# Attention with residual on one Trainium2 core: the second group's tokens turned by VectorE and DRAM, and one query product placed earlier

## The chip, the cores and the metric

The kernel runs on one core of a Trainium2 chip. A core has TensorE (PE in the profile, with its weight loads as PEld), VectorE (DVE), ScalarE (ACT), GpSimd (POOL) and SyncE (SP), which here only starts transfers. Each engine takes its instructions in a fixed order and waits where an operand is not ready. The metric is the time of one execution on the device in microseconds, as a median over runs; lower is better.

## The reference

Multi-query attention over 64 batches of 128 tokens with 512 features, 16 heads of 64, one shared key and value head and one extra "null" key and value per batch. A layer norm stands before and after; the input is added at the end.

```python
xn = layernorm(x, g_in)
q = (xn @ Wq).reshape(b, n, H, DH).transpose(0, 2, 1, 3) * scale
kv = xn @ Wkv
k, v = (kv[..., :DH], kv[..., DH:])
k = jnp.concatenate([nk, k], axis=1)      # null key, null value from cond_64
v = jnp.concatenate([nv, v], axis=1)
sim = jnp.einsum('bhid,bjd->bhij', q, k) + bias
sim = jnp.where(causal_mask, neg, sim)
sim = jnp.where(mask_p[:, None, None, :], sim, neg)
attn = jax.nn.softmax(sim, axis=-1)
out = jnp.einsum('bhij,bjd->bhid', attn, v)
out = out.transpose(0, 2, 1, 3).reshape(b, n, INNER)
return x + layernorm(out @ Wo, g_out)
```

Everything is float32.

## The kernel before

The 64 batches are worked in 16 groups of four (`GB = 4`, 512 tokens) and, for the attention itself, in 32 pairs. The instructions of each engine stand in the order in which the Python code issues them; nothing reorders them. So the lines at the end of the kernel (from line 1559) are a hand-written schedule, first for groups 0 and 1, then `body_first`, then a loop of `turn(d)` and `body(d)` over the pairs. A wait is set wherever an instruction needs a tile that another engine or a transfer writes, or a buffer that another still reads.

*Tokens.* The products need the normed tokens with features on partitions (`xT[g]`, one tile of 2048 columns for a group). There are two ways to get there:

- `norm_T(m)` (line 306), used for the tiles 0 to 7, that is for groups 0 and 1: the tile `x_m` holds one batch; TensorE turns its four 128x128 blocks into PSUM (line 313) and ScalarE copies them out in three pieces (line 315), with two of the four 32-token quarters exchanged.
- `tokens_T(m)`, `tokens_out(g)` and `tokens_in(g)` (lines 321 to 346), used from group 2 on: the tile `x_m` holds a quarter of the tokens of each of the four batches (the load at line 122 picks them). VectorE transposes all 32x32 blocks of the tile (line 326) into a quarter of `xb`, and when four tiles are done one transfer takes `xb` to DRAM (line 335) and four bring it back, 32 partitions each, as `xT` (line 343).

The statistics of a tile's tokens come from VectorE (`norm_stats`, with a power on POOL at line 281), and the norm itself from `norm_apply` (line 293), on ScalarE for the tiles 4 and up (line 302).

*Query products of group 0.* For each of 8 column blocks `c` of `wq` and each half `h` (two batches) of the group there is one product of four accumulating matrix multiplications, into one of two PSUM buffers, "a" for even `c` and "c" for odd. `q_half(c, h)` makes it 256 columns wide; `q_batches(cs)` does the same in two 128-column steps, one batch after the other, for `h = 0`. ScalarE copies the result to `qT` (line 459). The next product of the same parity waits for that copy.

*Bias and scores.* `causal(u)` masks half of the bias on POOL (line 212) and `null_shift(u)` subtracts the null bias on VectorE (lines 225 and 229). `bias_add(b)` on POOL (line 683) makes `s_b`, the bias and mask of a batch. `scores(b, 0)` goes to PSUM tiles of other stages, `scores(b, 1)` of batches 0 and 1 both to the one tile "s" of `ps_s` (line 718). `scores_add` on VectorE (lines 733 and 735) adds them to `s_b`, `scores_max` (line 740) takes maxima, `exps` on ScalarE (line 749) makes one exponential for each of 8 rows of a half, `rinv` (VectorE) and `scale` (POOL, line 771) divide, and `blocks_T` (VectorE, line 787) turns the 32x32 blocks for `values` (line 849).

*Group 1.* From group 1 on the query products are made by Strassen's method: `token_sum(g, k)` on POOL (line 497) and `weight_sum(k)` on VectorE (line 483) prepare sums, `product` (line 515) makes seven products. `body_first` (line 1091) issues those of group 1 for two column blocks `f` at once: after `kv_pair(4)` come the products 1, 2, 5, 6, 7, 4, 3, each for both `f`. Product 6 adds to the PSUM of product 1 and product 7 adds to that of product 6; between them ScalarE copies the running sum out (`keep`, line 527, tiles `kp1`, `ku2`, `ku3`). The order on ScalarE there is: copies of product 1, the keys of `kv_pair_out(4)` (line 390, behind VectorE's value part at line 380), `norm_apply(8)`, copies of product 6 (`ku2`), `norm_apply(9)`, copies of product 7 (`ku3`). `tokens_T(8)` and `tokens_T(9)` stand on VectorE between them.

*Transfers.* Nearly all are issued by SP, in code order. In the stage of the change these are: the value rows `vd` and `vr` (lines 406 and 411), the null value (line 189), the tiles 8 and 9 (line 122), the next mask, `wo` and `gob` (lines 238 and 239).

Of the kernel before, what the change touches and what calls it, by code (L numbers as in the profile page):

```python
# [17 lines left out]
def kernel(  # L18
# [96 lines left out]
    def load_x(m, queue=nc.sync):  # L115
        g, t = divmod(m, GB)
        pool, tag = (rp, "res") if m in (XB + 1, XB + 2) else (xp, "x")
        xs[m] = wM if m == XB else pool.tile([P, DIM], FP, tag=tag, name=f"x_{m}")
        if g < 2:
            queue.dma_start(out=xs[m], in_=x[m])  # L120
        else:
            nc.sync.dma_start(
                out=xs[m], in_=x[g * GB : (g + 1) * GB, t * Q : (t + 1) * Q, :]
            )
# [181 lines left out]
    def norm_T(m):  # L306
        g, t = divmod(m, GB)
        if t == 0:
            xT[g] = gp.tile([P, GB, KC, N], FP, tag="xT", name=f"xT_{g}")
        xh = xs.pop(m)  # L310
        pt = ps_w.tile([P, KC, P], FP, tag="w", name=f"pxT_{m}")
        for kc in range(KC):
            nc.tensor.transpose(pt[:, kc, :], xh[:, kc * P : (kc + 1) * P], ident)
        for at, to, n in ((0, 0, 2), (3, 2, 1), (2, 3, 1)):
            nc.scalar.copy(
                xT[g][:, t, :, to * Q : (to + n) * Q], pt[:, :, at * Q : (at + n) * Q]
            )
# [3 lines left out]
    def tokens_T(m):  # L321

        g, t = divmod(m, GB)
        if t == 0:
            xbs[g] = hp.tile([P, NQ, KC, NQ, Q], FP, tag="xb", name=f"xb_{g}", bufs=1)
        nc.vector.transpose(
            xbs[g][:, :, :, PLACE[t], :].rearrange("p j c q -> p c j q"),
            xs.pop(m).rearrange("p (c j k) -> p c j k", c=KC, k=Q),
        )
# [3 lines left out]
    def tokens_out(g):  # L333
        xds[g] = dp.tile([P, NQ, KC * NQ * Q], FP, tag="xd", name=f"xd_{g}")
        nc.sync.dma_start(
            out=xds[g], in_=xbs.pop(g).rearrange("p j c t q -> p j (c t q)")
        )

    def tokens_in(g):
        xT[g] = gp.tile([P, GB, KC, N], FP, tag="xT", name=f"xT_{g}")  # L340
        xd = xds.pop(g).rearrange("(i p) j e -> j p i e", p=Q)
        for j in range(NQ):
            nc.sync.dma_start(
                out=xT[g][j * Q : (j + 1) * Q].rearrange("p i c n -> p i (c n)"),
                in_=xd[j],
            )
# [81 lines left out]
    def q_tiles(g, fs, tags):  # L428
        units = [(f, h) for f in fs for h in range(2)]
        for (f, h), tag in zip(units, tags):  # L430
            qT[g, f, h] = gp.tile(
                [P, GB // 2, 2, 2, DH], FP, tag=tag, name=f"qT_{g}_{f}_{h}", bufs=1
            )
            q_tags[g, f, h] = tag
# [7 lines left out]
    def q_room(c, h):  # L442
        if c == 0 and h == 0:
            q_tiles(0, range(NF), [f"q{i}" for i in range(2 * NF)])
        return ps_q.tile([P, 2, N], FP, tag="ac"[c % 2], name=f"pq_{c}_{h}")

    def q_mm(pq, c, h, t=slice(0, 2)):
        two = slice(2 * h + t.start, 2 * h + t.stop)
        for kc in (0, 3, 2, 1):
            nc.tensor.matmul(  # L450
                pq[:, t],
                wq[:, kc, c * P : (c + 1) * P],
                xT[0][:, two, kc, :],
                start=(kc == 0),
                stop=(kc == 1),
            )

    def q_copy(pq, c, h):
        nc.scalar.copy(
            q_part(0, c, h), pq.rearrange("p t (h i) -> p t h i", h=2)  # L460
        )

    def q_half(c, h):
        pq = q_room(c, h)
        q_mm(pq, c, h)
        q_copy(pq, c, h)

    def q_batches(cs):
        pqs = [q_room(c, 0) for c in cs]
        for t in range(2):  # L470
            for pq, c in zip(pqs, cs):
                q_mm(pq, c, 0, slice(t, t + 1))
        for pq, c in zip(pqs, cs):
            q_copy(pq, c, 0)

    def weight_sum(k):
        o, p, m, op = {
# [7 lines left out]
    def token_sum(g, k):  # L485

        xS[g, k] = gp.tile([P, GB // 2, HK, N], FP, tag=f"xS{k}", name=f"xS{k}_{g}", bufs=1)
        lo, hi = xT[g][:, 0 : GB // 2], xT[g][:, GB // 2 :]
        b11, b12 = lo[:, :, lo_k], hi[:, :, lo_k]
        b21, b22 = lo[:, :, hi_k], hi[:, :, hi_k]  # L490
        p, m = {
            1: (b12, b11),
            2: (b22, xS.get((g, 1))),
            3: (b22, b12),
            4: (b21, xS.get((g, 2))),
        }[k]
        nc.gpsimd.tensor_tensor(xS[g, k], p, m, ALU.subtract)
# [178 lines left out]
    def bias_add(b, parts=(slice(0, ROW),)):  # L676
        g, t = divmod(b, GB)
        if b < B - 1:
            S[b] = sp.tile([P, R8, ROW], FP, tag="s", name=f"s_{b}", bufs=3)
        else:  # L680
            S[b] = hp.tile([P, R8, ROW], FP, tag="xb", name=f"s_{b}", bufs=1)
        for keys in parts:
            nc.gpsimd.tensor_tensor(  # L683
                S[b][:, :, keys],
                biasp[:, :, keys],
                mneg[:, t, keys]
                .unsqueeze(1)
                .broadcast_to([P, R8, keys.stop - keys.start]),
                ALU.add,
            )  # L690
# [46 lines left out]
    def scores_max(b, hf):  # L737
        if hf == 0:
            nmax[b] = small.tile([P, 2, R8], FP, tag="nmax", name=f"nmax_{b}")
        nc.vector.tensor_reduce(  # L740
            nmax[b][:, hf], S[b][:, :, WITH_NULL[hf]], AX.X, ALU.max, negate=True
        )

    def exps(b, hf, lo=0, hi=R8):
        if hf == 0 and lo == 0:
            rsum[b] = small.tile([P, 2, R8], FP, tag="rsum", name=f"rsum_{b}")
        for k in range(lo, hi):
            row = S[b][:, k, WITH_NULL[hf]]
            nc.scalar.activation(  # L749
                row,  # L750
                row,
                AF.Exp,
                bias=nmax[b][:, hf, k : k + 1],
                accum_out=rsum[b][:, hf, k : k + 1],
            )
# [848 lines left out]
    norm_apply(5)  # L1604
    q_batches((4,))
    norm_apply(6)
    norm_T(4)
    null_shift(1)
    causal(0)
    q_batches((5,))  # L1610
    norm_apply(7)
    norm_T(5)
    mask_neg(0)
    q_batches((6,))
    norm_T(6)
    null_shift(0)
    bias_add(0, (slice(0, UK.start), slice(UK.start, ROW)))
    q_half(7, 0)
    norm_T(7)
    load_null_value()  # L1620
    load_x(8)
    load_x(9)
# [6 lines left out]
    scores_add(0, 1)  # L1629
    scores_max(0, 1)  # L1630
    bias_add(2)
    exps(0, 0, 0, 4)
    q_half(0, 1)
    exps(0, 0, 4)
    q_half(1, 1)
    rinv(0, 0)
    scale(0, 0)
    token_sum(1, 1)
    token_sum(1, 2)
    scores(1, 0, ((ps_y, "X"), (ps_w, "w")))  # L1640
    scores(1, 1)
    scores_add(1, 0)
    scores_max(1, 0)
    scores_add(1, 1)
    scores_max(1, 1)
    exps(0, 1, 0, 4)
    q_half(2, 1)
    exps(0, 1, 4)
    rinv(0, 1)
    scale(0, 1)  # L1650
# [73 lines left out]
```

## Time and profile before

| | |
|---|---|
| median of 3 runs | 1023.34 us (1023.27 to 1023.65) |
| the profiled execution's own time | 1022.89 us |
| its span, first to last instruction | 1021.0 us |
| mean granted TensorE clock | 0.998 |
| transfers | 100.86 MB, mean 99 GB/s |

The busy time of an engine is given as us and as a share of the span; PE's matrix multiplications overlap each other and their ends are modelled. A row of a timeline gives start, length, engine, line, operation, output and inputs, how many instructions are merged into it, and in brackets the idle time ahead of it with what ended it. A row of the chain gives start, length and piece. All times count from the start of the span.

Over the first 120 us, taken in stretches of 10 us, PE is busy all of the time and POOL is busy 10.00, 9.92 and 10.00 us of the stretches from 30 to 60 us. Between 20 and 30 us VectorE is busy 6.33 us and ScalarE 7.74 us.

### The profile page before, as it was taken

To read this page: it belongs to the slowest core of one execution; us is meant where nothing else is said; L and a number is where in the kernel's file an instruction comes from. 1 tells how busy PE (TensorE), PEld (TensorE's weight loads), DVE (VectorE), ACT (ScalarE), POOL (GpSimd) and SP (SyncE) were. 2 spreads that over 40 slices of the span, in tenths; PEclk is the share of its full clock that TensorE was granted. 3 is DMA by queue.
4 is the path that set the end of the run, shared out by engine and by line. 5 is a ranking of instruction groups with operands and counts; after the bars stand their busy time and mean duration, and the time that the engine had idled before them with its cause. 6 is when DMAs were issued, how large, how long until landed. Compare 5 with 4: busy or idle time off the path is not lost.

```text
span 1021.0 us, 31459 instructions
## 1 busy us (share of the span) xinstructions
PE 1013.0 (99%) x12333; PEld 901.6 (88%) x12333; DVE 845.7 (83%) x1958; ACT 673.2 (66%) x2753; POOL 768.6 (75%) x633
## 2 busy tenths in 40 slices
PE   9999999999999999999999999999999999999997
PEld 9888888888888888888888888888988888888886
DVE  6777888888888888888888888888898888977787
ACT  5766677656677665686656776566775657865583
POOL 4997768677686877859678696776868768686686
PEclk9999999999999999999999999999999999999999
DMA  7415243151431415225152340514314152140221
GB/s 218 139 30 150 67 125 111 34 154 63 145 97 69 123 56 152 87 75 140 35 152 85 109 123 29 164 63 138 103 49 134 64 153 89 70 113 24 69 85 62
DMA packets 73835, 100.86 MB, mean 99 GB/s; under 512 B 32212, under 2 KB 36056, under 8 KB 71896
## 3 DMA queue, kind: packets, MB, share of 16 engines
q1 hardware_dynamic: 73392, 98.47, 32.3%
q8 instruction: 96, 1.57, 0.6%
q14 instruction: 51, 0.42, 0.1%
q10 hardware_dynamic: 296, 0.40, 0.1%
HBM read 63.19 MB, written 33.55 MB: 95 GB/s over the span
## 4 chain that ended last, share of the span: by engine, by line
PE 97%; POOL 1%; DVE 1%; issue 0%; ACT 0%; POOLq 0%; DVEq 0%
PE pyX L936 20%; PE pa L515 16%; PE pyY L936 10%; PE pc L515 10%; PE po L849 8%; PE pkv L363 6%; PE pyw L936 5%; PE pl L581 4%; PE pm L647 4%; PE ps L718 3%; PE pq L450 3%; PE sc_X L718 2%; PE sc_Y L718 2%; PE sc_a L718 1%; PE py_s L936 1%; PE busy L1556 1%
## 5 line engine op out<-in xcount | busy, mean ns | idle before, releaser
L749 ACT ACTIVATE s<-s,nmax 128x65 f32<-128x65 f32 (+1 forms) x1024 | 372.1, 369 | 61.7 <-DVE nmax L740 61.7
L771 POOL TENSOR_TENSOR s<-s,rinv 128x512 f32<-128x512 f32 (+1 forms) x132 | 190.6, 1446 | 132.7 <-DVE rinv L767 132.7
L683 POOL TENSOR_TENSOR s<-biasp,mneg 128x1552 f32<-128x1552 f32 (+1 forms) x65 | 206.3, 3177 | 51.0 <-DVE s L733 27.0
L749 ACT ACTIVATION_READ_ACCUMULATOR s<-s,nmax 128x1 f32 x1024 | 197.0, 192 | 0.0
L787 DVE STREAM_TRANSPOSE sb<-s 128x1536 f32<-128x1536 f32 (+1 forms) x68 | 113.6, 1674 | 11.3 <-POOL s L771 11.3
L740 DVE TENSOR_REDUCE nmax<-s 128x8 f32<-128x1032 f32 (+1 forms) x128 | 121.7, 951 | 0.1
L964 ACT COPY y<-pyX 128x256 f32<-128x256 f32 x29 | 10.8, 372 | 167.5 <-PE pyX L936 161.2
L936 PE MATMUL pyX<-wT,oT 128*128 128x256 f32 x464 | 109.8, 380 | 0.0
L936 PE MATMUL pyX<-wo,oT 128*128 128x256 f32 x464 | 109.7, 380 | 0.0
L936 PEld LDWEIGHTS pyX<-wo,oT 128*128 128x128 f32 x464 | 86.2, 191 | 10.4
L936 PEld LDWEIGHTS pyX<-wT,oT 128*128 128x128 f32 x464 | 84.2, 191 | 9.1
L916 POOL TENSOR_TENSOR oT<-oT 128x512 f32<-128x512 f32 x64 | 80.5, 1277 | 3.9 <-PE pyw L936 1.6
L527 ACT COPY ku<-pa 128x256 f32<-128x256 f32 x118 | 43.4, 367 | 59.7 <-issue 30.8
L849 PE MATMUL po<-sb,vr 32*64 32x128 f32 (+1 forms) x3904 | 81.8, 308 | 0.0
L849 PEld LDWEIGHTS po<-sb,vr 32*64 32x64 f32 x3904 | 71.4, 131 | 8.3 <-issue 5.9
L536 DVE TENSOR_TENSOR qT<-pc,ku 128x256 f32<-128x256 f32 x118 | 48.1, 408 | 32.2 <-PE pc L515 19.9
L868 ACT ACTIVATE oT<-po,nv 128x512 f32<-128x512 f32 (+1 forms) x127 | 73.5, 655 | 0.5 <-PE po L849 0.4
L515 PE MATMUL pa<-xS,wq 128*128 128x256 f32 x264 | 67.8, 380 | 0.0
L597 DVE TENSOR_TENSOR qT<-pl,kp 128x128 f32<-128x128 f32 x112 | 32.0, 286 | 42.8 <-PE pl L581 41.9
L281 POOL TENSOR_TENSOR rstd<-rstd,nhalf 128x1 f32<-128x1 f32 x64 | 35.2, 558 | 42.2 <-DVE rstd L280 39.3
L363 PE MATMUL pkv<-xT,wkv 128*128 128x256 f32 x256 | 63.4, 391 | 0.0
L515 PE MATMUL pa<-xT,wq 128*128 128x256 f32 x236 | 60.6, 380 | 0.0
(207 smaller groups left out, 2591.9 us busy)
## 6 DMA issues: line engine op xcount, KB each, us to landing
res<-in_x_dram SPq DMA_DIRECT2D x64, 256.0 KB
out_dram<-y SPq DMA_DIRECT2D x63, 256.0 KB
x<-in_x_dram SPq DMA_DIRECT2D x62, 256.0 KB
xd<-xb SPq DMA_DIRECT2D x14, 1024.0 KB
xT<-xd SPq DMA_DIRECT2D x56, 256.0 KB
vr<-vd SPq DMA_DIRECT2D x64, 128.0 KB
kT<-kT SPq DMA_DIRECT2D x32, 64.0 KB
vd<-vb SPq DMA_DIRECT2D x32, 64.0 KB
```

The lines of the kernel that those rows point to most:

```text
L363: nc.tensor.matmul(pkv, wkv[:, kc, :], xT[g][:, t : t + 2, kc, :], start=(kc == 0), stop=(kc == KC - 1),)
L515: nc.tensor.matmul(prod[tag], w[:, kc, f * P : (f + 1) * P], t[:, :, kc, :], start=(start and kc == 0), stop=(kc == HK - 1), skip_group_ch ...
L683: nc.gpsimd.tensor_tensor(S[b][:, :, keys], biasp[:, :, keys], mneg[:, t, keys] .unsqueeze(1) .broadcast_to([P, R8, keys.stop - keys.start ...
L718: nc.tensor.matmul(home[r][u * DH : (u + 1) * DH, f, :], qT[g, f, t // 2][rows, t % 2, hf, u], kT[rows, 0 : nk // Q, t, :], start=True, st ...
L740: nc.vector.tensor_reduce(nmax[b][:, hf], S[b][:, :, WITH_NULL[hf]], AX.X, ALU.max, negate=True)
L749: nc.scalar.activation(row, row, AF.Exp, bias=nmax[b][:, hf, k : k + 1], accum_out=rsum[b][:, hf, k : k + 1],)
L771: nc.gpsimd.tensor_tensor(sv, sv, rinvs[b, hf][:, lo:hi].unsqueeze(2).broadcast_to([P, hi - lo, sv.shape[2]]), ALU.mult,)
L787: nc.vector.transpose(sbs[b][:, :, lo:hi].rearrange("p j e q -> p e j q"), S[b][:, lo:hi, 1 : ROW - 1].rearrange("p e (j k) -> p e j k", k=Q),
L849: nc.tensor.matmul(po[s][rows, to : to + n], vr[g][quad, t, PLACE[j], :], sb[quad, slots, r * NF : (r + 1) * NF, :], start=(turn == 0), st ...
L868: nc.scalar.activation(to, src, AF.Identity, bias=nv2)
L916: eng.tensor_tensor(o, a, b, op)
L936: nc.tensor.matmul(prod[key], h[:, c, :], w[:, c, :], start=(start and c == 0), stop=(c == HC - 1), skip_group_check=not start,)
```

## The change

Three things change, all before `body_first`.

1. The tiles 4 to 7 of group 1 take the second way to `xT`. Their loads pick a quarter of the tokens of each batch (as those of the later groups do), `norm_T(4..7)` becomes `tokens_T(4..7)`, and `tokens_out(1)` and `tokens_in(1)` stand right behind the last of them, ahead of `null_shift(0)` in the code and ahead of `load_null_value`, `load_x(8)`, `load_x(9)` and `load_late` in SP's queue.
2. The product of block 2 for the second half of group 0, which stood between exponentials behind the scores of batch 1, stands ahead of those scores. The products of the blocks 0 and 1 are made in 128-column steps, and the first of them ahead of `exps(0, 0, 0, 4)`.
3. `token_sum(1, 1)` and `token_sum(1, 2)` stand some lines later in the code; on POOL, whose order they belong to, they keep their place between `scale(0, 0)` and `scale(0, 1)`.

```diff
-        if g < 2:
+        if g == 0:
             queue.dma_start(out=xs[m], in_=x[m])
         else:
             nc.sync.dma_start(
@@
-    def q_batches(cs):
-        pqs = [q_room(c, 0) for c in cs]
+    def q_batches(cs, h=0):
+        pqs = [q_room(c, h) for c in cs]
         for t in range(2):
             for pq, c in zip(pqs, cs):
-                q_mm(pq, c, 0, slice(t, t + 1))
+                q_mm(pq, c, h, slice(t, t + 1))
         for pq, c in zip(pqs, cs):
-            q_copy(pq, c, 0)
+            q_copy(pq, c, h)
@@
     norm_apply(6)
-    norm_T(4)
+    tokens_T(4)
     null_shift(1)
     causal(0)
     q_batches((5,))
     norm_apply(7)
-    norm_T(5)
+    tokens_T(5)
     mask_neg(0)
     q_batches((6,))
-    norm_T(6)
+    tokens_T(6)
+    tokens_T(7)
+    tokens_out(1)
+    tokens_in(1)
     null_shift(0)
     bias_add(0, (slice(0, UK.start), slice(UK.start, ROW)))
     q_half(7, 0)
-    norm_T(7)
     load_null_value()
@@
     bias_add(2)
+    q_batches((0,), 1)
     exps(0, 0, 0, 4)
-    q_half(0, 1)
+    q_batches((1,), 1)
     exps(0, 0, 4)
-    q_half(1, 1)
+    q_half(2, 1)
     rinv(0, 0)
     scale(0, 0)
-    token_sum(1, 1)
-    token_sum(1, 2)
     scores(1, 0, ((ps_y, "X"), (ps_w, "w")))
     scores(1, 1)
@@
     scores_max(1, 1)
+    token_sum(1, 1)
+    token_sum(1, 2)
     exps(0, 1, 0, 4)
-    q_half(2, 1)
     exps(0, 1, 4)
```

The functions that now serve group 1 as well are unchanged:

```python
    def tokens_T(m):
        ...
        nc.vector.transpose(
            xbs[g][:, :, :, PLACE[t], :].rearrange("p j c q -> p c j q"),
            xs.pop(m).rearrange("p (c j k) -> p c j k", c=KC, k=Q),
        )

    def tokens_out(g):
        xds[g] = dp.tile([P, NQ, KC * NQ * Q], FP, tag="xd", name=f"xd_{g}")
        nc.sync.dma_start(
            out=xds[g], in_=xbs.pop(g).rearrange("p j c t q -> p j (c t q)")
        )

    def tokens_in(g):
        ...
        for j in range(NQ):
            nc.sync.dma_start(
                out=xT[g][j * Q : (j + 1) * Q].rearrange("p i c n -> p i (c n)"),
                in_=xd[j],
            )
```

On TensorE, in the query products of group 0's first half (`pq`, the blocks 4 to 7), the order moves like this (`pxT` is the PSUM tile of the transposes, `wM` the tile of `x_4`, `x_202` to `x_206` those of the tiles 5 to 7; lines with + are the changed kernel's):

```order
 L450 MATMUL pq_0_388<-xT_175,wq 128x128 x8
-L313 MATMUL pxT_400<-wR,wM 128x128 x4
-L450 MATMUL pq_0_419<-xT_175,wq 128x128 x8
-L313 MATMUL pxT_430<-wR,x_202 128x128 x4
-L450 MATMUL pq_0_440<-xT_175,wq 128x128 x8
-L313 MATMUL pxT_450<-wR,x_204 128x128 x4
-L450 MATMUL pq_0_463<-xT_175,wq 128x256 x4
-L313 MATMUL pxT_469<-wR,x_206 128x128 x4
+L450 MATMUL pq_0_412<-xT_175,wq 128x128 x8
+L450 MATMUL pq_0_426<-xT_175,wq 128x128 x8
+L450 MATMUL pq_0_450<-xT_175,wq 128x256 x4
```

The 16 transposes are gone; the products follow each other directly, and the scores of batch 0 follow the last product.

On VectorE, between the norm factors of the tiles 5 to 7 and the scores of batch 0, the transposes stand around the two null shifts (`nbp` and `biasp`, lines 225 and 229):

```order
 L289 TENSOR_SCALAR nmr_385<-mv_340,rstd_342 128x1
+L326 STREAM_TRANSPOSE xb_399<-wM 128x4x4x32
 L225 COPY nbp<-nbh 64x8
 L229 TENSOR_TENSOR biasp<-biasp,nbp 64x8x192
+L326 STREAM_TRANSPOSE xb_399<-x_202 128x4x4x32
+L326 STREAM_TRANSPOSE xb_399<-x_204 128x4x4x32
+L326 STREAM_TRANSPOSE xb_399<-x_206 128x4x4x32
 L225 COPY nbp<-nbh 64x8
 L229 TENSOR_TENSOR biasp<-biasp,nbp 64x8x192
```

One transpose comes ahead of `null_shift(1)` and three come ahead of `null_shift(0)`.

In SP's queue, behind the value rows of group 0, the five transfers of the tokens come in:

```order
 L411 DMA vr_376<-vd_373 32x1024 x4
+L335 DMA xd_438<-xb_399 128x2048
+L343 DMA xT_440<-xd_438 32x4x512 x4
 L189 DMA nv_87<-in_cond_dram 64x1 x2
```

The null value and all that follows it in the queue is issued behind the wait of `tokens_in` for the transfer to DRAM.

## The prediction

> **What bounds the kernel now.** I read the page first: its busy shares and the shares of the chain that ended last.
>
> ```profile
> PE 1013.0 (99%) x12333; PEld 901.6 (88%) x12333; DVE 845.7 (83%) x1958; ACT 673.2 (66%) x2753; POOL 768.6 (75%) x633
> PE 97%; POOL 1%; DVE 1%; issue 0%; ACT 0%; POOLq 0%; DVEq 0%
> ```
>
> The chain is TensorE (PE) for 97% of 1021.0 us. So an instruction taken off PE is worth its length, unless PE then reaches something that is not ready. Next the chain in order of time, at the transposes the change removes (columns: start, length, piece).
>
> ```profile
> 22.52 0.43 PE pxT L313 x4
> 22.96 1.79 PE pq L450 x16
> ...
> 29.14 0.44 PE pxT L313 x4
> ...
> 31.07 3.65 PE pq L450 x16
> ...
> 35.35 0.88 PE ps L718 x32
> 36.23 10.56 PE pq L450 x48
> ```
>
> Four groups of transposes (the first and the last are shown) lie end to end with the query products. A product in 128-column pieces takes 1.79 us, one in 256-column pieces 10.56/6 = 1.76, and the two at 31.07 took 3.65.
>
> **What is removed.** 4 x 0.44 = 1.75 us of PE. ACT loses 12 PSUM copies, which frees only ACT. Two products become 128-column ones, 2 x (1.79 - 1.76) = 0.06 us more. If nothing else were late, PE would be 1.7 us ahead.
>
> **What is added on VectorE.** Four block transposes; their price is a row of the same instruction in a later group (the 54.42 row).
>
> ```profile
> 23.56 1.75 DVE L229 TENSOR_TENSOR biasp<-biasp,nbp 64x1536 f32<-64x1536 f32 x1 [1.16 <-POOL biasp L212]
> 25.33 0.53 DVE L225 COPY nbp<-nbh 64x8 f32<-64x8 f32 x1
> 28.06 1.75 DVE L229 TENSOR_TENSOR biasp<-biasp,nbp 64x1536 f32<-64x1536 f32 x1 [2.21 <-POOL biasp L212]
> 54.42 0.71 DVE L326 STREAM_TRANSPOSE xb<-x 128x512 f32<-128x512 f32 x1 [0.79 <-ACT x L302]
> ```
>
> ```profile
> 23.59 2.24 POOL L212 TENSOR_SCALAR_AFFINE_SELECT biasp<-biasp 64x512 f32<-64x512 f32 x1
> 26.94 1.09 POOL L212 TENSOR_SCALAR_AFFINE_SELECT biasp<-biasp 32x1024 f32<-32x1024 f32 x1
> 53.40 1.90 POOL L771 TENSOR_TENSOR s<-s,rinv 128x1024 f32<-128x1024 f32 x1
> 86.30 1.90 POOL L771 TENSOR_TENSOR s<-s,rinv 128x1024 f32<-128x1024 f32 x1 [2.31 <-DVE rinv L767]
> ```
>
> The first transpose (0.71) falls into the 1.16 us before the first null shift, the other three (2.13) into the 2.21 us before the second, where VectorE waits for POOL's causal select. From 25.31 (23.56 + 1.75) they end at 27.44, the copy of 0.53 at 27.97, under POOL's 28.03. The last needs `norm_apply(7)`:
>
> ```profile
> 25.05 0.81 ACT L302 ACTIVATE x<-x,nmr,rstd 128x512 f32<-128x512 f32 x1
> ```
>
> It ends at 25.86, and ACT now reaches it no later. So the transposes cost nothing as long as POOL's select covers them; the margin is 0.06 us. They do not slow POOL: the scale at 53.40 took 1.90 us across one, as did the scale at 86.30. But the small copy at 25.33 ended at 25.86, just after POOL's select (23.59 + 2.24 = 25.83): it seems to have waited for it. In its new place it meets the select that runs to 28.03, so the null shift starts up to 0.1 us late. At the far end, three transposes that all had to wait for POOL would end at 30.2, with the copy 30.7: 2.6 us late. The 54.42 row speaks against that; I take 0.05.
>
> [...]
>
> **The query product moved ahead** covers PE's next wait. The scores of batch 1, second half, need the PSUM that VectorE's add for batch 0 frees.
>
> ```profile
> 33.38 1.22 DVE L735 TENSOR_TENSOR s<-ps,s 128x1024 f32<-128x1024 f32 x1 [0.70 <-POOL s L683]
> ```
>
> That add ends at 34.60, and waits for POOL's bias, not for PE. PE used to reach those scores at 35.35. With 1.75 removed and one product (1.76) put ahead it reaches them near 35.4 again: no stall. Left where it was, the product would have left PE there near 33.6, 1.0 us early. Behind it, each product needs the PSUM copy of the one two before, and those copies stand between exponentials.
>
> ```profile
> 35.97 0.40 ACT L749 ACTIVATE s<-s,nmax 128x129 f32<-128x129 f32 x1
> ...
> 38.45 0.41 ACT L749 ACTIVATE s<-s,nmax 128x129 f32<-128x129 f32 x1
> ...
> 40.01 0.36 ACT L459 COPY qT<-pq 128x256 f32<-128x256 f32 x1
> ...
> 41.64 0.37 ACT L459 COPY qT<-pq 128x256 f32<-128x256 f32 x1
> ```
>
> Four long exponentials take 40.01 - 38.45 = 1.56 us, a copy with the four short ones behind it 41.64 - 40.01 = 1.63. ACT used to start the eight long ones at 35.97, with a copy and a wait among them. Now they run through to 35.97 + 3.12 = 39.1, and product 3 is copied by 39.5; PE wants that buffer at 36.2 + 2 x 1.76 = 39.7. The later copies (by 41.1, 42.8 and 44.6, with the steps above) come 0.4 us or more before PE wants theirs (41.5, 43.2, 46.7). If ACT were 0.5 us slower there, PE would stall, but PE has 1.3 us to lose there before the end notices (below).
>
> **Where the lead is lost.** Ahead of PE's second pair of kept products stands a chain that starts with POOL and VectorE and that the change does not move: transposed blocks of batch 0, a weight sum, the values, then ACT.
>
> ```profile
> 48.20 1.77 DVE L787 STREAM_TRANSPOSE sb<-s 128x1536 f32<-128x1536 f32 x1
> ...
> 52.35 0.49 DVE L380 TENSOR_SCALAR vT<-pkv,nkv 64x256 f32<-64x256 f32 x1
> ```
>
> ```profile
> 52.92 0.76 ACT L390 ACTIVATE kT<-pkv,nkv 64x128 f32<-64x128 f32 x3 [2.27 <-DVE vT L380]
> 53.58 0.81 ACT L302 ACTIVATE x<-x,nmr,rstd 128x512 f32<-128x512 f32 x1
> 54.59 0.37 ACT L527 COPY ku<-pa 128x256 f32<-128x256 f32 x1 [0.20 <-PE pa L515]
> ...
> 56.44 0.36 ACT L527 COPY ku<-pa 128x256 f32<-128x256 f32 x1
> ```
>
> ```profile
> 55.42 0.86 PE pa L515 x4
> 57.14 0.90 PE pa L515 x4
> ```
>
> ```profile
> 56.91 0.73 PEld L515 LDWEIGHTS pa<-xS,wq 128*128 128x128 f32 x4 [0.17 <-issue]
> ```
>
> `body_first` queues on ACT: keys, `norm_apply(8)`, then the copy of `u2`. PE's product 7 adds to the same PSUM and must wait for that copy. The copy waited only 0.20 us for PE, so it can move up by 0.20 (to 54.39) or, if ACT overlaps instructions as at 55.72 to 56.44, to about 54.30. It then ends at 54.67 to 54.76. From the 56.44 copy's end (56.80) PE's weight load began 0.11 later and its product counted from 57.14, 0.34 in all. So product 7 starts at 55.01 to 55.10 instead of 55.42: the 1.7 us shrink to 0.3 or 0.4, and PE waits some 1.3 us there. With the 0.05 of VectorE, **a gain of 0.3 us stays**. Behind this point everything hangs on PE again: POOL, full until then, has 2.80 us to spare.
>
> ```profile
> 82.09 1.90 POOL L771 TENSOR_TENSOR s<-s,rinv 128x1024 f32<-128x1024 f32 x1 [2.80 <-DVE rinv L767]
> ```
>
> **The tokens through DRAM.** SyncE's queue gets five transfers behind the values' four, and the null value, two `x` tiles and the output weights wait behind them.
>
> ```profile
> 26.40 1.73 SPq L411 DMA_DIRECT2D vr<-vd  x4
> 80.03 0.33 SPq L335 DMA_DIRECT2D xd<-xb  x1
> 83.92 0.33 SPq L343 DMA_DIRECT2D xT<-xd  x1
> 88.16 0.63 SPq L406 DMA_DIRECT2D vd<-vb  x1
> 89.24 2.61 SPq L406 DMA_DIRECT2D vd<-vb  x1
> ```
>
> In a later group the way out took 83.92 - 80.03 = 3.9 us; the two `vd` issues waited for the first two returning pieces, so these landed about 4.2 and 5.3 us after 83.92 and the fourth, at 1.1 us a piece, near 7.5. From 28.2 (26.40 + 1.73) that makes 39.6. The reader is POOL's token sum:
>
> ```profile
> 40.63 2.28 POOL L497 TENSOR_TENSOR xS<-xT 128x512 f32<-128x512 f32 x1
> 42.98 2.13 POOL L497 TENSOR_TENSOR xS<-xT,xS 128x512 f32<-128x512 f32 x1
> 45.08 2.88 POOL L771 TENSOR_TENSOR s<-s,rinv 128x1024 f32<-128x1024 f32 x1
> ```
>
> So the trip is hidden with 1 us to spare. PE's own use comes at 36.23 + 10.56 - 1.7 = 45.1, and of the transfers queued behind the first are the `x` tiles, which VectorE reads only after that.
>
> **Sum.** -1.75 + 0.06 + 1.3 + 0.05 = about -0.3 us, made against the profiled execution (1022.89 us, span 1021.0; the median is 1023.34, 0.45 above): **1023.0 us** on the median.
>
> **Rivals.** *The whole lead survives* (0.13): VectorE's chain to the values comes 1.3 us earlier than I think, because ACT finishes the exponentials sooner. For it: ACT has fewer copies. Against it: from 48.20 on the rows lie back to back and start with POOL's scale, not with ACT. It gives 1023.34 - 1.7 = 1021.6. *The null shift slips* (0.12): a transpose more than 0.06 us longer pushes bias, scores and the chain above, and each us of slip is lost one to one; between 0.5 and 1 us this is 1023.5 to 1024.0, in the 2.6 us limit 1025.6. *The tokens land late* (0.07), the slower case: at a landing T POOL needs about 2 x 1.28 + 1.90 us more to finish the scale that VectorE's 48.20 row waits for, with no competing rows by then; it decides from T = 43.5, and T = 45 gives 1023.0 + 1.5 = 1024.5, T = 47 gives 1026.5. Against it: 39.6 is 4 us away. *The change does nothing for PE* (0.03): 1023.3; the order of the instructions shows the transposes gone.
>
> **How the numbers follow.** My forecast, 1022.7 to 1023.3, has 0.65. The range 1021.5 to 1024.4 takes in the surviving lead below and most slips above; beyond it I leave the longest slips and late tokens. A measurement of this kernel tells about 0.2%, 2.05 us, from no change. Faster by more than that needs more than the 1.7 us that are there: 0.05. Slower by more needs the far ends of two rivals: 0.08. Within: 0.87.
>
> **What would show it.** PE's `pxT` rows after 22 us are gone; the scores of batch 0 start near 27.8; the causal null shift starts at 28.1; the copy `ku` at 54.3 to 54.4 follows `norm_apply(8)` with no wait for PE, and PE shows an idle gap of about a microsecond before the seventh product near 55. No such gap, or one in the forties, proves the account wrong; so does a token sum that waits for a transfer.

## The result, and the profile after

| | before | changed kernel |
|---|---|---|
| median, runs side by side (4 and 4) | 1023.48 us (1023.27 to 1023.65) | 1037.68 us (1037.18 to 1040.02) |
| the profiled execution's own time | 1022.89 us | 1037.43 us |
| its span | 1021.0 us | 1035.6 us |
| ratio of the runs | | 1.0143, 95% interval 1.0130 to 1.0156 |

The change costs 14.2 us, 1.4%, far outside the predicted range of 1021.5 to 1024.4.

The page of the changed kernel first: busy shares and the shares of the chain. TensorE's busy time is 3 us longer although it has the same 12333 instructions, and the chain, 97% TensorE before, now has 3% transfers in it.

```profile
PE 1016.0 (98%) x12333; PEld 901.6 (87%) x12333; DVE 846.4 (82%) x1962; ACT 671.1 (65%) x2741; POOL 765.9 (74%) x633
PE 92%; DMA 3%; DVE 2%; POOL 1%; issue 1%; ACT 1%; SPq 0%; POOLq 0%; DVEq 0%; ACTq 0%
```

What TensorE waits for in the changed kernel (line waited for, total us, times, longest). The first three rows are new.

```profile
PE pa L515 <- ACT ku L527: 4.9, 1, 4.9
PE pq L450 <- ACT qT L459: 4.0, 2, 3.4
PE sc_Y L718 <- ACT qT L459: 2.1, 1, 2.1
```

ACT is the releaser only by name, so I followed the wait backwards. First stage, in the changed kernel's timeline of VectorE, ScalarE and POOL (brackets: idle time ahead and what ended it):

```profile
18.08 0.69 DVE L270 BATCH_NORM_STATS2 st<-x 128x6 f32<-128x512 f32 x1 [0.43 <-DMA x<-in_x_dram]
...
20.86 0.69 DVE L270 BATCH_NORM_STATS2 st<-x 128x6 f32<-128x512 f32 x1 [1.68 <-DMA x<-in_x_dram]
...
23.91 0.14 DVE L373 TENSOR_SCALAR nkv<-nkv 64x1 f32<-64x1 f32 x1 [1.95 <-DMA nkv<-in_cond_dram]
```

```profile
24.62 0.76 ACT L390 ACTIVATE kT<-pkv,nkv 64x128 f32<-64x128 f32 x3 [6.12 <-DVE vT L380]
```

```profile
25.68 2.05 PE L450 MATMUL pq<-xT,wq 128*128 128x128 f32 x16 [3.38 <-ACT qT L459]
```

VectorE waits for the tiles of group 1 and then for the null key, a tiny transfer that stands behind those tiles in SP's queue and is issued at 11.56 us in place of 8.83; ScalarE stands 6.12 us behind VectorE with the query copies queued behind its keys; TensorE finds no free PSUM at 22.3. The windows of the same time show why the transfers are late (columns: stretch, length, busy time and count of PE, PEld, DVE, ACT, POOL, granted clock, share of the 16 DMA engines, GB/s). The changed kernel, then the kernel before:

```profile
12.00:14.00 2.00, 2.00 (x20) 2.00 (x19) 0.78 (x2) 0.50 (x2) 0.00 (x0) 1.00 0.34 123
14.00:16.00 2.00, 2.00 (x17) 1.90 (x16) 0.72 (x2) 1.50 (x7) 0.00 (x0) 1.00 0.35 115
```

```profile
12.00:14.00 2.00, 2.00 (x20) 2.00 (x19) 1.20 (x3) 0.72 (x2) 0.00 (x0) 1.00 1.05 389
```

Same bytes to load, a third of the engines at work; the rate for a full share is alike (123/0.34 = 362 GB/s against 389/1.05 = 370), so fewer engines move, and not slower ones. Second stage, around the seventh product, in the changed kernel:

```profile
53.75 0.69 DVE L270 BATCH_NORM_STATS2 st<-x 128x6 f32<-128x512 f32 x1 [3.48 <-DMA x<-in_x_dram]
...
58.19 0.69 DVE L270 BATCH_NORM_STATS2 st<-x 128x6 f32<-128x512 f32 x1 [3.34 <-DMA x<-in_x_dram]
...
59.21 1.77 DVE L787 STREAM_TRANSPOSE sb<-s 128x1536 f32<-128x1536 f32 x1
...
63.27 0.49 DVE L380 TENSOR_SCALAR vT<-pkv,nkv 64x256 f32<-64x256 f32 x1
```

```profile
63.85 0.76 ACT L390 ACTIVATE kT<-pkv,nkv 64x128 f32<-64x128 f32 x3 [7.87 <-DVE vT L380]
```

```profile
59.72 1.03 PE L515 MATMUL pX<-xS,wS 128*128 128x256 f32 x4
65.67 2.04 PE L515 MATMUL pa<-xS,wq 128*128 128x256 f32 x4 [4.92 <-ACT ku L527]
67.51 1.91 PE L515 MATMUL pX<-xS,wq 128*128 128x256 f32 x4
...
72.20 1.03 PE L515 MATMUL pc<-xT,wS 128*128 128x256 f32 x4
```

```profile
60.00:70.00 10.00, 5.08 (x14) 3.85 (x13) 5.76 (x11) 3.45 (x9) 10.00 (x6) 0.75 0.21 64
```

VectorE waits 3.48 and 3.34 us for the tiles 8 and 9; behind them, in the order of its code, stand the blocks of batch 0, the weight sum and the values for ScalarE's keys. TensorE stands 4.92 us. Its granted clock is 0.75 on the mean of these ten us; in windows of 1 us it is 1.00 up to 64 us and 0.50 from 65 to 71, and a product takes 1.91 us in place of 1.03.

The ledger: TensorE's idle gaps are 3.38, 0.65 and 2.15 us in the first stage. At the keys of group 1 (line 363, 46.62 us before) the changed kernel is 5.33 us behind; the three gaps less the 1.75 us of transposes would make 4.4, and the other 0.9 is not taken apart. The gap of 4.92 follows. From 65.67 to 72.20 the four products take 6.53 us where 4 x 0.86 = 3.44 would do (0.86 is the step from one start to the next at 58.86 and 59.72), 3.1 more. That makes 13.35; the first value product (line 849, 63.52 us before) is 13.46 us behind. By 160 us it is 13.8, and so it stays through the loop.

### The profile page after: what moved, and what is told of

Its sections match the earlier page's. It is cut to its first block, busy times and chain, and to the rows that moved or that the text cites. A ratio compares the mean times of both kernels' runs of the same rounds, so it can differ in the third digit from the quotient of the medians.

```text
span 1035.6 us, 31459 instructions
## 1 busy us (share of the span) xinstructions
PE 1016.0 (98%) x12333; PEld 901.6 (87%) x12333; DVE 846.4 (82%) x1962; ACT 671.1 (65%) x2741; POOL 765.9 (74%) x633
## 4 chain that ended last, share of the span: by engine, by line
PE 92%; DMA 3%; DVE 2%; POOL 1%; issue 1%; ACT 1%; SPq 0%; POOLq 0%; DVEq 0%; ACTq 0%
PE pyX L936 19%; PE pa L515 15%; PE pyY L936 10%; PE pc L515 10%; PE po L849 8%; PE pkv L363 5%; PE pyw L936 5%; PE pl L581 4%; PE pm L647 4%; PE ps L718 3%; PE sc_X L718 2%; PE sc_Y L718 2%; DMA x<-in_x_dram 1%; DMA nkv<-in_cond_dram 1%; PE sc_a L718 1%; PE pq L450 1%
## 5 line engine op out<-in xcount | busy, mean ns | idle before, releaser
L515 PEld LDWEIGHTS pa<-xS,wq 128*128 128x128 f32 x264 | 50.9, 194 | 12.5 <-issue 5.3
```

The costliest lines, as they stand in the source:

```text
L515: nc.tensor.matmul(prod[tag], w[:, kc, f * P : (f + 1) * P], t[:, :, kc, :], start=(start and kc == 0), stop=(kc == HK - 1), skip_group_ch ...
```

## The experiments

The kernels of the experiments 1 to 6 were run once each, beside the kernel before at 1022.96 us (1 to 4, one run) or 1023.57 us (5 and 6, median of 9, from 1023.12 to 1025.13), so a difference of a microsecond or two in them is no more than a hint; the others have medians of 4 to 11 runs.

**1 and 2: the form of the loads, in the kernel before.** Tiles 4 to 7 are still one batch each, but the rows are read in 4 pieces of 32, or in 16 pieces of 8 (`n = 16`).

```diff
+        if g == 1:
+            rows, n = x.rearrange("b n e -> (b n) e"), 4
+            each = P // n
+            some = rows[m * P : m * P + n * (each + 1)]
+            some = some.rearrange("(i p) e -> i p e", i=n)[:, 0:each]
+            nc.sync.dma_start(out=xs[m], in_=some)
```

> The kernel before, but the tiles 4 to 7 are loaded as 4 pieces of 32 rows each, with one row skipped between pieces (the same bytes, almost the same place; the output differs, since the tiles hold other rows). Theory 1, the form of the load: a load whose outer dimension is 4 keeps only 4 of 16 DMA engines busy, so the four tiles, the null key and the bias come late as in the changed kernel. In the changed kernel the first bias add started 5.9 us late; expected here 1027 to 1030 us, a DMA share near 0.35 between 12 and 20 us. Theory 2, the trip through DRAM alone is what costs: 1023.0 to 1023.8 us.

> The same, but 16 pieces of 8 rows with one row skipped between pieces (the output differs likewise). If the number of pieces decides (theory 1): 1023.0 to 1023.8 us, DMA share near 1.0 between 10 and 14 us. If it is that the rows do not lie in one run: late as with 4 pieces, 1027 us or more.

Measured: 1029.66 us with 4 pieces, 1023.56 with 16, both as the first theory had it. The windows of the two kernels, 4 pieces first:

```profile
10.00:20.00 10.00, 10.00 (x78) 9.59 (x77) 5.73 (x16) 3.87 (x11) 2.20 (x4) 1.00 0.48 167
20.00:30.00 10.00, 7.01 (x45) 6.78 (x44) 5.57 (x15) 4.40 (x15) 4.62 (x7) 0.74 0.37 95
```

```profile
10.00:20.00 10.00, 10.00 (x77) 9.59 (x76) 7.63 (x22) 4.35 (x14) 3.04 (x5) 1.00 0.98 220
20.00:30.00 10.00, 10.00 (x114) 9.58 (x116) 6.43 (x12) 8.06 (x27) 7.71 (x7) 1.00 0.46 89
```

Nothing differs but the number of pieces that the outer dimension of the read has (and, with it, which rows are skipped). With 4 the DMA share is half (0.48 against 0.98) and TensorE loses 3.0 us by a gap and more by the clock (0.74 from 20 to 30 us); with 16 it is busy throughout. So 6 us of loss need neither transposes nor a trip.

**3: the changed kernel with the loads of tiles 4 to 7 as before** (`if g < 2` at line 119).

> The changed kernel, but the tiles 4 to 7 are loaded as before, one whole batch each (the transposes then put the tokens elsewhere, so the output differs). Theory 1: the stalls of PE before 40 us are gone and the first bias add starts near 30.0 again; what stays is the tiles 8 and 9, which are issued behind the trip and, on 4 engines, land about 14 and 22 us after the transfer to DRAM is issued at 28.2, so VectorE waits about 3 us for the second: 1024 to 1027 us. Theory 2: still 1030 us or more.

Measured: 1028.95 us, between the two theories. The first stage is mended: the scores of batch 0 start 1.81 us earlier than before, the keys of group 1 1.52 us earlier. So the lead that the prediction counted on is there. What is left is the second stage. The first theory had named the tiles 8 and 9, but with a wait of about 3 us; VectorE waits 2.29 and 3.46 us, and TensorE has one gap of 4.4 us and the slow clock behind it (0.93 from 50 to 60 us and 0.90 from 60 to 70, products of 1.78 and 1.91 us). In this kernel's timeline of VectorE:

```profile
46.30 0.69 DVE L270 BATCH_NORM_STATS2 st<-x 128x6 f32<-128x512 f32 x1 [2.29 <-DMA x<-in_x_dram]
...
50.85 0.69 DVE L270 BATCH_NORM_STATS2 st<-x 128x6 f32<-128x512 f32 x1 [3.46 <-DMA x<-in_x_dram]
```

**4: the move of the query product alone, in the kernel before.**

```diff
+    q_batches((0,), 1)
     exps(0, 0, 0, 4)
-    q_half(0, 1)
+    q_batches((1,), 1)
     exps(0, 0, 4)
-    q_half(1, 1)
+    q_half(2, 1)
```

> The kernel before with only the second part of the change: the product of block 2 ahead of batch 1's scores, the blocks 0 and 1 in 128-column steps, the token sums where the change has them. Theory 1: it neither gains nor costs by itself, 1023.0 to 1023.9 us, since PE reaches batch 1's scores 1.7 us later with the same work. Theory 3, the new order of products and copies starves PE: 1025 us or more.

Measured: 1028.84 us, 5 us above the first theory. The third has the number, but not its mechanism: near the edit only 0.8 to 1.6 us were lost (by the starts of the first value product and of the keys behind it). The rest came in small waits of TensorE all along the run, with nothing that the profile shows as releaser. Of the rows below the one at `pa` is another matter, the gap before the seventh product, which the next experiment has too:

```profile
PE pkv L363 <- issue: 1.6, 6, 0.4
...
PE pa L515 <- issue: 0.7, 1, 0.7
PE po L849 <- issue: 0.6, 1, 0.6
```

**5: the same move with 256-column products**, so that TensorE gets as many matrix multiplications as before (`q_half(0, 1)` and `q_half(1, 1)` in the new places).

> The kernel before with the product of block 2 ahead of batch 1's scores, but blocks 0 and 1 made 256 columns wide as before, so that TensorE executes as many instructions as before. The run with 128-column steps had 16 more matmul records, came out at 1028.8 us and lost its time in small stalls without a visible releaser, all along the run. Theory 3a, the count of TensorE's instructions shifts where its instruction stream stalls: 1023.0 to 1024.3 us here, with no such stalls (the later scores of batch 1 may cost up to 1.3 us). Theory 3b, the order itself costs: 1027 us or more.

Measured: 1025.02 us, 0.7 above the expectation; the small waits along the run are gone. There is one gap of 0.8 us before the seventh product; the first value product starts 0.92 us late, and the one run is 1.5 us above the median before. Without a lead of TensorE the moved product delays the scores of batch 1 (36.78 us in place of 35.17) and all that VectorE does behind them.

**6: the changed kernel with whole-batch loads for the tiles 4 to 9** (`if m < 10` at line 119).

> The changed kernel with whole-batch loads for the tiles 4 to 9 (the output differs), everything else in its place, the tiles 8 and 9 still behind the trip through DRAM. If the form of the loads is what makes the tiles 8 and 9 late (4 of 16 DMA engines): VectorE no longer waits for them, PE's stall of 4.4 us before product 7 shrinks to the 1.3 to 2 us of the prediction, 1022.4 to 1023.8 us. If it is their place in the queue, behind the trip and beside the output weights: 1027 us or more.

Measured: 1025.33 us, between the two ranges. VectorE now waits 0.58 us for the tiles 8 and 9 in place of 6.8, though they stand as late in the queue as in the changed kernel: it was their form more than their place. But 1.8 us are left. In this kernel's timelines:

```profile
28.15 0.37 SPq L335 DMA_DIRECT2D xd<-xb  x1
34.80 1.74 SPq L343 DMA_DIRECT2D xT<-xd  x4
```

```profile
44.34 1.28 POOL L497 TENSOR_TENSOR xS<-xT 128x512 f32<-128x512 f32 x1 [3.98 <-DMA xT<-xd]
45.70 1.27 POOL L497 TENSOR_TENSOR xS<-xT,xS 128x512 f32<-128x512 f32 x1
46.92 1.91 POOL L771 TENSOR_TENSOR s<-s,rinv 128x1024 f32<-128x1024 f32 x1
```

```profile
48.86 1.78 DVE L787 STREAM_TRANSPOSE sb<-s 128x1536 f32<-128x1536 f32 x1 [2.09 <-POOL s L771]
...
50.88 2.30 DVE L483 TENSOR_TENSOR wq<-wq 128x1024 f32<-128x1024 f32 x1
53.21 0.49 DVE L380 TENSOR_SCALAR vT<-pkv,nkv 64x256 f32<-64x256 f32 x1
```

The way out takes 6.65 us from issue to the next issue, and the tokens land at 44.3. POOL stands 3.98 us, its scale ends late, VectorE's blocks wait for it, and the values come at 53.21 where they came at 52.35 before. TensorE stands 1.7 us before the seventh product, which starts 0.36 us later than before instead of 0.3 to 0.4 earlier. This is the mechanism of the prediction's third rival, which was to decide from 43.5 on. Its size is smaller than the loss: for 44.3 the rival's formula gives 1023.8. By the trace 0.39 us are lost at the first value product and 1.7 by 160 us; what is lost between is not taken apart. In the changed kernel itself POOL stands 3.83 us before the same token sum, behind a way out of 6.0 us.

**7: the same tokens, with loads that avoid four pieces.** Tiles 4 to 7 come as four transfers of 32 partitions, one for each batch; tiles 8 and 9 as eight transfers of 32 rows, between the way out and the way back.

```diff
-        for m in range(4, 8):
-            load_x(m)
+        four = wS[:, 0:2].rearrange("p a k f -> p (a k) f")
+        for r in range(GB):
+            nc.sync.dma_start(
+                out=four[r * Q : (r + 1) * Q],
+                in_=x[GB + r].rearrange("(t q) e -> q t e", q=Q),
+            )
@@
     tokens_out(1)
+    load_rows(8)
+    load_rows(9)
     tokens_in(1)
```

> The changed kernel with the same tokens loaded in another form: the tiles 4 to 7 by four transfers, one for each batch, of 32 rows of partitions and four pieces of 512 (into the space of the weight sums, which is free then), the statistics of tile 4 a few instructions later; the tiles 8 and 9 by eight transfers of 32 rows, issued while SP waits for the transfer to DRAM. If the form of these loads is the whole loss: the first bias add starts within 0.5 us of the kernel before and the time is 1022.6 to 1024.0 us, about the prediction's. If the trip itself costs more: 1026 us or more.

Measured: 1031.14 us (1030.77 to 1031.45), ratio 1.0071 (1.0056 to 1.0086). A miss: the number lies with the second theory, but the loss stands in the first stage again, where TensorE has a gap of 3.55 us. In this kernel's windows and VectorE's timeline:

```profile
10.00:12.00 2.00, 2.00 (x20) 2.00 (x20) 1.49 (x5) 0.37 (x1) 1.33 (x2) 1.00 1.07 380
12.00:14.00 2.00, 2.00 (x21) 2.00 (x20) 1.15 (x2) 0.37 (x1) 0.00 (x0) 1.00 1.07 161
14.00:16.00 2.00, 2.00 (x16) 1.90 (x15) 1.13 (x3) 1.66 (x8) 0.00 (x0) 1.00 1.05 215
```

```profile
19.96 0.69 DVE L285 BATCH_NORM_STATS2 st<-wS 128x6 f32<-128x512 f32 x1 [3.81 <-DMA biasp<-in_fside_16xSxS_dram]
```

All 16 engines are at work (1.07), but they move 161 to 215 GB/s instead of 389: with transfers of 32 partitions each, the packets take longer here. In the trace a packet of 2048 bytes takes 157 to 212 ns on the mean from 12 to 16 us, and 88 to 93 in the kernel before. And the first statistics need all four transfers, so they start at 19.96. (The row names a transfer of the bias as what ended the wait; the instruction reads the loaded tiles, and in the eighth kernel the same wait is put down to them.)

**8: the same, with the blocks of batch 0 behind ScalarE's chain.**

```diff
             product(g, f, 2, ps_w, "w")
             q_out(g, f, 0, "w", "p1" + "'" * f)
+        blocks_T(0)
         tokens_T(m)
@@
     scale(1, 0)
     q_half(5, 1)
-    blocks_T(0)
```

> The run before this one with one more edit: the block transposes of batch 0 stand behind the values' copy and the first two query outputs of group 1 on VectorE, instead of ahead of the third weight sum. The prediction's chain to product 7 then no longer passes through POOL's scale and 1.77 us of transposes. If that chain is what eats the lead: PE's gap before product 7 is gone or under 0.3 us and the time is 1.0 to 1.7 us below the run before this one (1021.4 to 1022.6 us). If not: the same as that run.

Measured: 1029.18 us (1029.14 to 1030.26), 1.96 below the seventh experiment, a little more than expected. The gap before the seventh product is 0.21 us where it was 1.43. So the chain that the prediction named, blocks, weight sum, values, keys, copy, is what TensorE waits for there, and the blocks can leave it. Of the difference in time only this 1.2 us can be put down to the edit: in the two profiled executions the loads of the first stage differ too, and the eighth kernel is 1.50 us ahead at the keys of group 1 already, in front of the edit.

**9 to 11: no load in four pieces, every token in its place, and the move on and off.** The diff is an excerpt. Tiles 4 to 7 are loaded whole; group 1 works on an `xT` whose outer index is the quarter of the tokens; tiles 8 and 9 come in rows and the blocks stand late.

```diff
+            raw[g] = gp.tile([P, NQ, GB, KC, Q], FP, tag="xT", name=f"xT_{g}")
+            xT[g] = raw[g].rearrange("p i t c q -> p t c i q")
@@
+            for at, to, n in ((0, 0, 2), (3, 2, 1), (2, 3, 1)):
+                nc.sync.dma_start(
+                    out=xds[g][to * Q : (to + n) * Q], in_=xb[at * Q : (at + n) * Q]
+                )
```

> The changed kernel with the output of the reference and with no load in four pieces in this stage: the tiles 4 to 7 are loaded as whole batches, as in the kernel before, and VectorE, the trip and the token sums of group 1 work on a layout in which the quarter of the tokens is the outer index of xT (the way out becomes three transfers, which exchange two quarters); the tiles 8 and 9 come as 8 transfers of 32 rows between the way out and the way back; the transposed blocks of batch 0 stand behind the first two outputs of body_first. Theory 1 (all of the loss is the form of the loads, plus the chain of VectorE ahead of the seventh product, plus the token sum behind the trip): no wait for x before the query products, PE's gap ahead of the seventh product under 0.5 us, 1021.8 to 1023.2 us if before is 1023.5, so up to 1.7 below it. Theory 2 (the query product placed ahead of the scores, or the trip, costs by itself in a way that this order does not reach): 1024.5 to 1026, with a gap of 1 us or more somewhere between 40 and 60 us.

> The same kernel without the second part of the change: the query products of the second half stand where the kernel before has them. If what the move alone cost (about 1.5 us) was the delay that it brings to the scores of batch 1 while PE has no lead to spend on it, then here, where PE has the lead of the removed transposes, the move is worth something: without it PE waits about 1.0 us before the scores of batch 1 at about 34 us, as the prediction has it, and the time is 0 to 1.0 above the kernel with the move. If the move costs in any order, the time is 0.5 to 1.5 below the kernel with the move.

> Control: the kernel before, with nothing but the transposed blocks of batch 0 moved behind the first two outputs of body_first. PE does not wait there in the kernel before, so the edit alone should be worth nothing: within 0.3 us of the kernel before. A gain of 1 us or more would say that what it brought behind the changed kernel's loads was no matter of the lost lead.

Measured, beside 1023.64 us of the kernel before: 1025.26 (ratio 1.0014, 1.0005 to 1.0023), 1031.56 (1.0079, 1.0063 to 1.0095) and 1023.63 (0.9998, 0.9990 to 1.0007). The control is worth nothing, as expected. The first of the three fell on its second theory, and the second came out 5 us above its range. What TensorE waits for in the ninth kernel, and its POOL's timeline:

```profile
PE pa L555 <- POOL xS L524: 1.2, 1, 1.2
```

```profile
45.31 1.27 POOL L524 TENSOR_TENSOR xS<-xT 128x512 f32<-128x512 f32 x1 [5.02 <-DMA xT<-xd]
```

The scores of batch 0 start 2.1 us earlier than before (0.35 of it TensorE has from its first 10 us on) and the keys of group 1 1.3; then the seventh product waits 1.2 us for a token sum on POOL, which waited 5.02 us for the trip. By the first value product the kernel is 0.12 us behind the one before; another 1.3 go in small steps up to 160 us, which are not taken apart. About 0.6 of this may belong to the one profiled execution of the kernel before, which is 0.45 us under its median: the control, whose median is that of the kernel before, loses 0.6 to 0.7 against it on the same stretch. The kernel without the move had the 1.1 us wait that the prediction had worked out (1.0), and besides the small waits of the fourth experiment:

```profile
PE po L889 <- issue: 1.7, 5, 0.6
...
PE ps L758 <- DVE s L775: 1.1, 1, 1.1
```

**12: what brings the small waits.**

```diff
-    q_half(0, 1)
+    q_batches((0,), 1)
@@
-    q_half(1, 1)
+    q_batches((1,), 1)
```

> The kernel without the query product moved ahead (c2_whole_fixed_no_q_move), with one edit: the products of the blocks 0 and 1 of the second half are made in 128-column steps where they stand, as the change makes them, so that TensorE gets 16 more matrix-multiplication records and has 12333 again, as in the kernel before, in place of 12317. So far the scattered waits of TensorE with no releaser ('issue', 0.1 to 0.7 us each, all along the run) stood in the two kernels whose count is another one, 12349 (a4_q_move_alone) and 12317, and in none with 12333. Theory 1 (the waits come with the number of TensorE instructions ahead of the loop, whatever is moved): they go, and what is left against c1_whole_fixed is the stall of about 1.1 us before the scores of batch 1, so 1024.5 to 1026.5 us. Theory 2 (they come with the missing move, by the times at which things happen): they stay, 1029 us or more.

Measured: 1024.94 us (1023.91 to 1025.93) beside 1023.44; ratio 1.0015 (1.0006 to 1.0024). Sixteen more matrix multiplications in the same place made the kernel 6.6 us faster. The small waits are gone:

```profile
PE ps L758 <- DVE s L775: 1.4, 1, 1.4
...
PE pa L555 <- POOL xS L524: 0.4, 1, 0.4
```

The waits without a releaser in the tenth kernel, whose profiled execution is its slowest (1034.74 us), make up 2.1 us only. The rest is inside TensorE's busy time, nearly all at the value products. The tenth kernel's row, then the twelfth's (count, busy time, mean of one in ns, idle time):

```profile
L889 PE MATMUL po<-sb,vr 32*64 32x128 f32 (+1 forms) x3904 | 88.9, 309 | 2.1 <-issue 1.7
L889 PE MATMUL po<-sb,vr 32*64 32x128 f32 (+1 forms) x3904 | 81.9, 308 | 0.0
```

The same 3904 products are busy 7.0 us longer, at the same length of one: their weight loads stand 11.4 us without a releaser (46 times, at most 0.9), in the twelfth kernel 5.7 (32 times, at most 0.3).

With the move (ninth) TensorE waits 1.2 us before the seventh product; without it (twelfth) 1.4 before the scores and 0.4 before the product. The two medians, against their own runs of the kernel before, are not told apart (1.0014 and 1.0015). None of the kernels tried is faster than the one before; with good loads the change comes out 1.6 us slower, and 1.5 without the move.

## Why the prediction was wrong

*The step that failed* is one it did not take: the new loads were priced at nothing. The change was listed part by part as transposes, trip and product; that the tiles 4 to 7 take the form of line 122 is told in the part on the change and has no term in the sum. With the old loads put back (third experiment), about 8.5 us of the 14.2 go (1037.43 to 1028.95, one run); the form of the loads alone cost the kernel before 6.1 us (first and second, 1029.66 to 1023.56). The rows were there to be read. In the kernel before, two tiles of that form are issued at 54.44, and nothing else of size is in flight:

```profile
54.44 1.14 SPq L122 DMA_DIRECT2D x<-in_x_dram  x2
```

```profile
54.00:56.00 2.00, 2.00 (x11) 1.77 (x10) 0.71 (x1) 1.30 (x4) 2.00 (x2) 1.00 0.25 39
56.00:58.00 2.00, 2.00 (x11) 1.65 (x10) 0.84 (x3) 1.17 (x3) 2.00 (x1) 1.00 0.25 60
```

A share of 0.25 is 4 of 16 engines. At 60 GB/s a tile of 256 KB (262 thousand bytes) takes 4.4 us; the gaps between the statistics of the tiles 8 and 9 after the change (53.75 to 58.19) are 4.4 us. With four batches outermost the share was 0.25 here and 0.34 and 0.35 in the changed kernel from 12 to 16 us; with 16 pieces it was 0.98 in the second experiment. That the number of pieces sets it is what the first two experiments show for 4 and 16; for other numbers no run does.

*The tiles 8 and 9.* "[...] of the transfers queued behind the first are the `x` tiles, which VectorE reads only after that" priced their delay at nothing as well. They were issued at 45.13 in place of 29.39, and two slow tiles need about 8.7 us; VectorE stood 6.8 us for them in its fixed order. The third and the sixth experiment, one run each, give 3.6 us for it (1028.95 to 1025.33; 4.2 if each is taken against the kernel before beside it).

*The trip* was mis-sized. 39.6 was worked out with 3.9 us for the way out and 7.5 for the way back, from a later group. In the sixth experiment they took 6.65 and 9.5, and the tokens landed at 44.3; in the ninth, with more transfers between, at 45.3. The value rows ahead explain only a part of the longer way out: in the sixth kernel the DMA share is 0.82 and 0.96 from 28 to 32 us and then 0.09 up to 34, one or two engines of 16, and why these are late stays open. The rival of late tokens, at a chance of 0.07, was the one that a kernel with good loads meets, and the sign that the prediction named against itself, a token sum that waits for a transfer, stands in all of these kernels. That it gave 1024.5 for 45 and 1025.26 was measured is partly chance: in the ninth kernel the blocks are out of the rival's chain, and most of the loss lies behind the first value product.

*The lead* was right: 1.75 us off TensorE. With the old loads the scores of batch 0 come 1.81 us early, 0.07 of it from the first 20 us. *The transposes on VectorE* were right too, and the null shift late by about 0.1: in the third kernel,

```profile
23.09 1.76 DVE L229 TENSOR_TENSOR biasp<-biasp,nbp 64x1536 f32<-64x1536 f32 x1 [1.08 <-POOL biasp L212]
24.87 1.90 DVE L326 STREAM_TRANSPOSE xb<-x 128x512 f32<-128x512 f32 x3
26.70 0.88 DVE L225 COPY nbp<-nbh 64x8 f32<-64x8 f32 x1
27.66 1.75 DVE L229 TENSOR_TENSOR biasp<-biasp,nbp 64x1536 f32<-64x1536 f32 x1
```

the three take 1.90 us against 2.13 in the sum, the copy takes 0.88 us against 0.53 before and ends at 27.58, just behind POOL's select (27.54), and the shift starts at 27.66. The first shift is 0.47 us earlier there than before (23.09 against 23.56), so 27.66 stands against 28.06 - 0.47 = 27.59.

*Where the lead is lost* was the right place: the seventh product waited for `ku` behind the values in the changed kernel, the third and the sixth, and in the eighth moving the blocks took 1.2 us off its gap. But it was lost for another reason as well, the token sum, and so moving the blocks does not save it. *The product moved ahead* was right in its 1.0 us: without it TensorE waits 1.1 to 1.4 us before the scores of batch 1. In the kernel before, where there is no lead, the move alone came out 1.5 us slower in its one run, 0.9 of it at the first value product.

The range failed because no rival was about the loads. The one that was about transfers asked when the trip ends; none asked whether a load would move at the rate of the one that it replaces.

## What to carry to other kernels

When a load changes its pattern, price it like an instruction: look in the trace for a transfer of that very form and read its DMA share. A form that did no harm where the tiles issued at 54.44 are read only at 68.53 cost 6.1 us at the start (1029.66 against 1023.56), where the first statistics wait for it and small transfers stand behind it. And follow a late transfer through the fixed order of the engine that waits: here two waits for tiles of a later group held up the values of this one.

## What the runs showed of the hardware that was not expected

- A load whose outer dimension is 4 ran at a DMA share of 0.25 to 0.35 and 60 to 123 GB/s; the stage with the same number of bytes in 16 pieces ran at 0.98 over ten microseconds, where it was 0.48 with 4.
- Transfers to 32 partitions at a time ran at a full share, 1.07 and 1.05, and 161 and 215 GB/s in the seventh kernel from 12 to 16 us, where the loads of whole batches ran at 1.05 and 389 GB/s in the kernel before (12 to 14 us). Why the same share moves about half the bytes is not shown.
- A gap of TensorE cost more than its length in some kernels and not in others: after 4.92 us idle the granted clock was 0.50 for some 7 us (0.75 over 10 us) and products took 1.91 us; after 3.0 us in the first experiment it was 0.74 over 10 us; after 3.38 us in the changed kernel and 3.55 in the seventh it stayed 1.00.
- TensorE stalled all along the run, 0.1 to 0.6 us at a time in its own rows and up to 0.9 at its weight loads, with no releaser, in the two kernels with 12349 and 12317 matrix multiplications, and not in the twelve with 12333, which show at most two such waits of 0.3 us at `po` (and in three of them one before the seventh product, where the copy `ku` is what is late). The twelfth experiment restored the count and the stalls went. The form of the products is not the cause: 128-column steps stand on the slow side of one pair (fourth and fifth) and on the fast side of the other (tenth and twelfth). The two pairs point to the count, or to where the instructions come to lie by it; that is not shown by more than these pairs, and how it works stays open. In these pairs 16 instructions more or fewer came with 3.8 us (1028.84 against 1025.02) and 6.6 us (1031.56 against 1024.94), so a part of a change tried alone misled here.
